# Pairing messages of one bin into double rows before the scatter, in one group of five, in a graph kernel on one core

## The chip, the core and the metric

The kernel runs on one core of a Trainium2 chip. The metric is the device time of one execution in microseconds (us); the figure used is the median of several runs. One further execution is recorded by the hardware profiler; all views below come from it.

## The reference

A graph layer with N = 12,500 nodes of 128 features and 400,000 edges. An edge has a source node `src`, a target `dst` (sorted), 20 attributes and a weight. Cut to what matters:

```python
h    = maximum(layernorm(x), 0) @ W_in2f.T            # one row per node
Wij  = (smu(edge_attr @ W_f1.T + b_f1) @ W_f2.T + b_f2) * edge_weight[:, None]
x_ij = h[dst] * Wij                                   # one message of 128 per edge
agg  = segment_sum(x_ij, src, num_segments=N)         # sum of messages by source node
out  = x + smu(agg @ W_o1.T + b_o1) @ W_o2.T + b_o2
```

`smu` is a smooth activation (Gelu plus a linear part). Edges come sorted by `dst`, so the rows of `h` that a tile needs lie close together; the sum, though, goes by `src`, which is random.

## The kernel before, in words

**Tiles, groups, supers.** 128 edges are a tile, four tiles a group (`GRP`), two groups a super; 3,125 tiles make 782 groups and 391 supers. The nodes are cut into 98 bins of 128.

**Two phases, overlapped.** In the first phase each message is written to a slot of its bin in DRAM: a row of 129 floats (128 values and the node's place within the bin), by one indirect DMA per tile, issued by GpSimd (`scatter_tile`, L812 to L821; the instruction is recorded at L815). In the second phase the slots of a bin are read back 128 rows at a time (`fetch`, L839), VectorE compares the places with a row of numbers to make a 0/1 matrix (`choose`, L860), and TensorE adds all messages of a node by an f32 product with it (`add`, L873); VectorE adds the result to `agg` (L886).

**Parts.** The supers are cut into ten parts (`PARTS`, L33), each with its own capacity per bin (`CAP`, a multiple of 128, from the mean plus 5.8 deviations) and three DRAM buffers used in turn. While the messages of part k are computed and scattered, the slots of part k-1 are read back and summed: `chores` and `parts` spread those products evenly over the groups of the part. With the parts of before, the capacities are 6, 6, 6, 6, 5, 4, 3, 3, 2 and 1 times 128, 42 in all. The first part also carries the setup (layer norm, `h`, weight splitting), as `step` deals it out.

**Kept groups.** The supers of the last two parts (from 368 on, `EARLY`; 23 of them) are computed early, one after every nine others, from the second part on, and their rows are kept in DRAM (`kept_rows`). At the end they are only loaded and scattered. So the first 368 supers are the scattered ones of the main loop (736 groups), and from about 3,700 us on only kept rows are scattered.

**A round.** The main loop (from L1324) has a round per group. The order on each engine is written out by hand; in the round of position p:

- `send(g)` scatters group p (GpSimd, in order), at the top of the round
- `number(p+1)` (L641, VectorE) makes the slot indices; `weigh(p+1)` (L741, L742, TensorE) makes the filter rows into the one `pw` bank
- the first half of the bin sums (L873)
- `mix(p+1)`: ScalarE writes the places (`places_in`, L802 or L804), VectorE multiplies filter and gathered rows into a message buffer `ms` (L754); there are six of them, and one is free again when the scatters that read it have landed
- `gather`, `take` (L697, L716), `hide`, `bend` (L661, L669) and `pick_part` (L552, L553) for groups p+2 and p+3
- `count(p+2)` (L599 to L602, TensorE), `bins(p+3)` (L585, VectorE), `read(p+2)` (L629, VectorE): the slot number of a message is its rank among the messages of its bin. `bins` builds 0/1 rows of 98 bins that are summed along the tiles, `count` adds up within a tile with a triangular matrix, and `read` picks a message's own count by a maximum
- the second half of the bin sums

SyncE issues the loads and the reads of the slots in its own order. Should a count exceed a capacity, a flag in `bad` sends the kernel into a slow repair path at its end.

Of the kernel before, what the change touches and what calls it, by code (L numbers as in the profile page):

```python
# [32 lines left out]
PARTS = (59, 59, 59, 59, 48, 37, 27, 20, 16, 7)  # L33
# [6 lines left out]
ROUND = 12582912.0  # L40


@with_exitstack
def gnn_kernel(
# [46 lines left out]
    for a, n in eps_of:  # L91
        mean = n * SUP * P * P / N
        dev = SIGMA * math.sqrt(mean)
        CAP.append(math.ceil((mean + dev) / P) * P)
        ZMIN.append(max(0, math.floor((mean - dev) / ZP) * ZP) if len(ZMIN) < BUFS else 0)
# [4 lines left out]
    assert all(NB * c < 1 << 24 and c < BIG - 1 for c in CAP)  # L100
# [6 lines left out]
    stores = [dram.tile([NB * CAP[k], ROW], F32, name=f"buf{k}") for k in range(min(BUFS, EPOCHS))]  # L107
    bufs = [stores[k % BUFS][0:NB * CAP[k], :] for k in range(EPOCHS)]
    tab = dram.tile([N + P, D], F32, name="tab")
# [51 lines left out]
    bad = const.tile([P, 4 + 2 * EPOCHS], F32, name="bad")  # L161
# [24 lines left out]
    wls = const.tile([P, P], BF, name="wls")  # L186

# [123 lines left out]
    with tc.tile_pool(name="ld", bufs=4) as ld, \  # L311
# [40 lines left out]
        def head_of(c):  # L352
# [7 lines left out]
            rb = parts_tile().rearrange("p n k d -> p (n k d)").bitcast(U8)[:, :GRP * P].rearrange("p (n e) -> p n e", e=P)  # L360
            z = 0 if c else FEW
            base_f = edge.tile([1, CH // GRP], F32, name="base_f")
# [62 lines left out]
        ds = edge.tile([P, FEW], I32, name="ds", bufs=1)  # L425
        ss = edge.tile([P, FEW], I32, name="ss", bufs=1)
        dsf = edge.tile([P, FEW], F32, name="dsf", bufs=1)
        ssf = edge.tile([P, FEW], F32, name="ssf", bufs=1)
# [67 lines left out]
        loaded, onehot, bins_of, slots, hidden, taken = {}, {}, {}, {}, {}, {}  # L496

# [23 lines left out]
        def targets(s):  # L521
# [3 lines left out]
            rb = ld.tile([P, SUP * P], U8, name="rbc")  # L525
# [39 lines left out]
        def bins(g):  # L565
# [6 lines left out]
            so = cnt.tile([P, GRP, NB], F16, name="so_kept" if kept else "so", bufs=2 if kept else 3)  # L572
# [11 lines left out]
            for j in range(n):  # L584
                nc.vector.scalar_tensor_tensor(so[:, j], irow_ps[:, :NB], hi_f[:, t + j:t + j + 1],  # L585
                                               so[:, j - 1] if j else before, op0=ALU.is_equal, op1=ALU.add)
            last[k] = so[:, n - 1]
            bins_of[g] = (before, so)
# [3 lines left out]
        def count(g):  # L592
# [3 lines left out]
            n = groups[g][1]  # L596
# [3 lines left out]
            if n > 1:  # L600
                nc.tensor.matmul(pc[:, 1:n], rest_h, so[:, :n - 1], start=False, stop=False, skip_group_check=True)  # L601
# [1073 lines left out]
```

## Time and profile before

| | |
|---|---|
| median of 3 runs | 4070.55 us (4062.09 to 4072.97) |
| the profiled execution's own time | 4075.27 us |
| its span in the trace | 4073.5 us |
| indirect scatters | 2944 of computed rows at L815, 181 of kept rows |
| bytes moved by DMA | 891.06 MB |
| mean granted TensorE clock | 0.922 |

The span is the time from the first to the last recorded instruction; the execution's own time lies 1.8 us above it. In the views, PE is TensorE, PEld its weight loads, DVE VectorE, ACT ScalarE, POOL GpSimd. A row of the lines reads: line, engine, operation, output<-inputs, shapes, count, then busy time in us and the mean duration of one in ns, then the idle time of the engine just before them and what ended it. Busy time counts overlapping instructions once, so busy time over count can be less than the mean duration. In the waits, the row names who waited, for whom, the us in total, the times and the longest.

### The profile page before, as it was taken

How to read it: one execution, taken by the hardware profiler on the slowest of the kernel's cores; microseconds unless marked ns; L12 is line 12 of the kernel's file. 1: busy time of each engine (PE TensorE's matmuls, PEld its weight loads, DVE VectorE, ACT ScalarE, POOL GpSimd, SP SyncE). 2: the span in 40 equal slices, each digit the busy share in tenths (PEclk: the TensorE clock that was granted, in tenths of full speed). 3: DMA queues.
4: the chain of work that ended last, by engine and by line, in shares of the span. 5: the costliest groups of instructions: out<-in, count | busy, mean ns of one | idle time of the engine just before them, and what ended most of it. 6: DMA issues, size and time to landing. Idle time of an engine off the chain costs nothing.

```text
span 4073.5 us, 78743 instructions
## 1 busy us (share of the span) xinstructions
PE 3198.0 (79%) x23721; PEld 2666.9 (65%) x24048; DVE 2964.6 (73%) x6883; ACT 2723.2 (67%) x6848; POOL 3066.0 (75%) x3169
## 2 busy tenths in 40 slices
PE   7767767878888788788887788888788788888658
PEld 4345555666667666666766667777677677777547
DVE  7986666777777777777777777777777777777347
ACT  6769877777777677777777777777666666665002
POOL 6777767777777777777777777777777777777776
PEclk9978888998999999989999999999989999989889
DMA  5887778888887767767777768777777877877888
GB/s 163 240 238 198 214 206 241 244 235 234 242 245 217 204 196 216 204 203 207 208 207 220 204 195 231 216 218 221 212 203 216 223 209 226 229 208 200 254 251 252
DMA packets 659740, 891.06 MB, mean 219 GB/s; under 512 B 183268, under 2 KB 460904, under 8 KB 659178
## 3 DMA queue, kind: packets, MB, share of 16 engines
q1 hardware_dynamic: 551881, 666.59, 59.6%
q0 software_dynamic: 100112, 207.06, 15.8%
q10 hardware_dynamic: 7312, 12.29, 0.9%
q8 instruction: 191, 3.13, 0.3%
q14 instruction: 244, 1.99, 0.2%
HBM read 500.66 MB, written 384.95 MB: 217 GB/s over the span
## 4 chain that ended last, share of the span: by engine, by line
DMA 33%; PE 17%; POOL 15%; DVE 15%; issue 11%; ACT 8%; SPq 0%; DVEq 0%; ACTq 0%; POOLq 0%; another core or an unknown queue 0%
DMA buf<-ms,ix 31%; POOL buf L815 15%; PE pw L741 6%; PE pg L873 5%; DVE ms L754 4%; DVE so L585 4%; ACT hg L716 3%; DVE sl L629 1%; DVE se L860 1%; PE ph L697 1%; ACT oh L552 1%; PE pw L742 1%; ACT ge L669 1%; ACT oh L553 1%; PE pc L599 1%
## 5 line engine op out<-in xcount | busy, mean ns | idle before, releaser
L815 POOL DMA_INDIRECT buf<-ms,ix x2944 | 2850.4, 968 | 929.1 <-issue 644.6
L741 PE MATMUL pw<-w_f,ge 128*128 128x128 f32 x5568 | 1099.9, 322 | 501.1 <-DVE ms L754 461.6
L873 PE MATMUL pg<-se,rw 128*128 128x128 f32 x8036 | 1244.4, 296 | 143.4 <-DVE se L860 81.0
L741 PEld LDWEIGHTS pw<-w_f,ge 128*128 128x128 f32 x5568 | 915.6, 207 | 613.0 <-DVE ms L754 433.1
L873 PEld LDWEIGHTS pg<-se,rw 128*128 128x128 f32 x8036 | 1062.6, 203 | 230.6 <-issue 105.1
L754 DVE TENSOR_TENSOR ms<-pw,hg 128x512 f32<-128x512 f32 x696 | 479.3, 689 | 736.8 <-DMA buf<-ms,ix 442.2
L585 DVE SCALAR_TENSOR_TENSOR so<-irow_ps,hi_f,so 128x98 f16<-128x98 f32 x2936 | 931.5, 317 | 78.1
L716 ACT ACTIVATE hg<-ph,w_sb 128x128 f32<-128x128 f32 x2784 | 789.5, 365 | 281.5 <-PE ph L697 272.2
L860 DVE TENSOR_TENSOR se<-irow_ps,rw 128x1536 f32<-128x1536 f32 (+1 forms) x345 | 588.0, 1704 | 148.9 <-DMA rw<-buf 120.2
L742 PE MATMUL pw<-wls,f 128*128 128x128 bf16 x2784 | 642.4, 231 | 0.0
L553 ACT ACTIVATE oh<-oh,onesb 128x512 bf16<-128x512 bf16 x780 | 562.7, 721 | 25.4
L552 ACT ACTIVATE oh<-rbc,nrow 128x512 bf16<-128x512 uint8 x762 | 564.6, 741 | 4.0 <-DMA rbc<-rel_dram 4.0
L629 DVE TENSOR_REDUCE sl<-pc 128x4 f32<-128x392 f32 x782 | 434.9, 556 | 7.1 <-PE pc L602 6.4
L802 ACT ACTIVATE ms<-lo_b,mark 128x4 f32<-128x4 bf16 (+1 forms) x428 | 125.6, 293 | 443.1 <-DMA buf<-ms,ix 417.6
L697 PE MATMUL ph<-hw,oh 126*128 126x128 bf16 x2784 | 294.1, 232 | 64.0 <-ACT oh L553 55.0
L742 PEld LDWEIGHTS <-f 128*128 128x128 bf16 x2784 | 295.4, 106 | 0.0
L697 PEld LDWEIGHTS <-oh 126*128 126x128 bf16 x2784 | 204.1, 104 | 134.8 <-ACT oh L553 119.5
L669 ACT ACTIVATE ge<-pu 128x512 f32<-128x512 f32 x450 | 274.5, 610 | 14.4 <-PE pu L661 13.7
L599 PE MATMUL pc<-so,tri 128*128 128x392 f16 x736 | 255.3, 347 | 24.3 <-DVE sl L629 4.6
L601 PE MATMUL pc<-so,rest_h 128*128 128x294 f16 x736 | 221.2, 300 | 0.0
L815 POOL DMA_INDIRECT buf<-ms,ix_kept x181 | 175.0, 967 | 55.2 <-issue 54.0
L804 ACT ACTIVATE ms<-lo_b 128x4 f32<-128x4 bf16 x353 | 72.4, 205 | 205.8 <-DMA buf<-ms,ix 190.7
(266 smaller groups left out, 2867.2 us busy)
## 6 DMA issues: line engine op xcount, KB each, us to landing
rw<-buf SPq DMA_DIRECT2D x292, 774.0 KB
f<-f_parts SPq DMA_DIRECT2D x370, 240.0 KB
buf<-zero SPq DMA_DIRECT2D x146, 387.0 KB
rbc<-rel_dram SPq DMA_DIRECT2D x389, 128.0 KB
buf<-ms,ix POOLq DMA_INDIRECT x2944
f_parts<-hs SPq DMA_DIRECT2D x105, 360.0 KB
rw<-buf SPq DMA_DIRECT2D x49, 645.0 KB
f_parts<-hs SPq DMA_DIRECT2D x107, 240.0 KB
```

The costliest lines, as they stand in the source:

```text
L552: nc.scalar.activation(oh, loaded[s][1][:, o:o + n], AF.Abs, bias=pneg if s < FEW // SUP else nrow)
L553: nc.scalar.activation(oh, oh, AF.Relu, scale=-1.0, bias=onesb[:, 0:1])
L585: nc.vector.scalar_tensor_tensor(so[:, j], irow_ps[:, :NB], hi_f[:, t + j:t + j + 1], so[:, j - 1] if j else before, op0=ALU.is_equal, op1 ...
L629: nc.vector.tensor_reduce(sl[:, :n], pc[:, :n], op=ALU.max, axis=AX.X)
L697: nc.tensor.matmul(ph[:, j * P:(j + 1) * P], oh[:3 * WIN, a:a + P], hw[:3 * WIN, g % PER, :], start=True, stop=True)
L716: nc.scalar.activation(hg[:, j * P:(j + 1) * P], rows_of[g][:, j * P:(j + 1) * P], AF.Copy, scale=w_sb[:, t + j:t + j + 1])
L741: nc.tensor.matmul(pw[:, a:a + P], ge[:, a:a + P], w_f2, start=True, stop=False)
L742: nc.tensor.matmul(pw[:, a:a + P], fb[:, o + a:o + a + P], wls, start=False, stop=True)
L754: nc.vector.tensor_tensor(ms[:, :n, 0:P], pw.rearrange("p (j f) -> p j f", f=P)[:, :n], hg.rearrange("p (j f) -> p j f", f=P)[:, :n], op=A ...
L815: i = nc.gpsimd.indirect_dma_start(out=bufs[k][:, :], out_offset=bass.IndirectOffsetOnAxis(ap=ix[:, j:j + 1], axis=0), in_=ms[:, j, :], in ...
L860: nc.vector.tensor_tensor(se[:, a:a + n], own.unsqueeze(1).to_broadcast([P, n, P]), rows_in[c][:, a:a + n, P:P + 1].to_broadcast([P, n, P] ...
L873: nc.tensor.matmul(pgs[0][:, g, :], rows_in[c][:, o, 0:P], sel[c][:, o, :], start=(q == 0), stop=(q == Q[k] - 1))
```

## The change

In one group of five (a *paired* group), the messages of tiles 2 and 3 are not scattered as they are. Each looks for a row of tile 0 or 1 of the same bin and the same rank within its bin; if there is one, it moves, by a product with a 0/1 matrix, into a second half of that row. The rows of tiles 0 and 1 then have 258 floats and go to two neighbouring slots, by one indirect DMA for each of the two tiles. The messages of tiles 2 and 3 that found no row (*leftovers*) are gathered by a third 0/1 matrix into one tile of 128 rows, which is scattered with a later group, its *host*, at least four positions on. So a paired group issues two scatters, its host five. A row without a partner has zeros in its second half.

What changes with it:

- the plan of pairs; the parts become 56, 56, 56, 56, 46, 36, 36, 26, 16, 7, and the capacities allow for more slots: 6, 6, 6, 6, 5, 4, 4, 3, 2, 1 times 128. The rows of the main loop stay the first 368 supers.
- `bins`, `count`, `read`, `number`: in a paired group the ranks of tiles 0 and 1 count double, and tiles 2 and 3 are ranked by themselves; one more row of bins in paired and host groups; a fifth count in the host
- new functions `spread_keys`, `match`, `rank_left`, `place_left`, `permute`, `take_pairs`, called in the rounds p and p+1
- `mix` splits the product of a paired group in two and writes places, bins and slot bases for the moved half
- fewer buffers: `rbc` 3 instead of 4, `mt` 2 of 6 x 128 columns instead of 3 of 4 x 128; the head's small tiles share others

The diff, cut to its core:

```diff
-PARTS = (59, 59, 59, 59, 48, 37, 27, 20, 16, 7)
+PARTS = (56, 56, 56, 56, 46, 36, 36, 26, 16, 7)
+EVERY = 5
+WIDER = 0.17
...
+        for p, g in enumerate(seq):
+            if g // PER >= EARLY:
+                continue
+            since_pair += 1
+            if wanting and p >= wanting[0][0] + 4:
+                host[g] = wanting.pop(0)[1]
+            elif since_pair >= EVERY and g > BY and g + 10 < ends_of[epoch[g // PER]]:
+                paired[g] = len(paired)
+                wanting.append((p, g))
+                since_pair = 0
...
+            if g in paired:
+                last[k] = so[:, GRP]
+                nc.vector.scalar_tensor_tensor(so[:, GRP], so[:, 1], 2.0, before, op0=ALU.mult, op1=ALU.add)
+            if g in host:
+                last[k] = so[:, GRP]
+                nc.vector.scalar_tensor_tensor(so[:, GRP], irow_ps[:, :NB], left_of[host[g]][1], so[:, GRP - 1],
+                                               op0=ALU.is_equal, op1=ALU.add)
...
+            if g in paired:
+                nc.tensor.matmul(pc[:, :n], tri2, so[:, :n], start=True, stop=False, skip_group_check=True)
+                nc.tensor.matmul(pc[:, 1:n:2], both2, so[:, 0:n:2], start=False, stop=False, skip_group_check=True)
+                nc.tensor.matmul(pc[:, :n], ones_h, before.unsqueeze(1).to_broadcast([P, n, NB]), start=False, stop=True,
+                                 skip_group_check=True)
...
+        def spread_keys(g):
+            kt = ps1.tile([P, GRP * P], F32, name="pt")
+            for j in range(2):
+                nc.tensor.transpose(kt[:, j * P:(j + 1) * P], keys_of[g][:, j:j + 1].to_broadcast([P, P]), ident)
...
+        def match(g):
+            kt, key = matched[g], keys_of.pop(g)
+            pp = edge.tile([P, 6 * P], F32, name="mt", bufs=2)
...
+            for i in range(2):
+                nc.vector.scalar_tensor_tensor(pp[:, i * 2 * P:(i + 1) * 2 * P].rearrange("p (j e) -> p j e", j=2),
+                                               kt[:, :2 * P].rearrange("p (j e) -> p j e", j=2), key[:, 2 + i:3 + i],
+                                               onesb.unsqueeze(1).to_broadcast([P, 2, P]),
+                                               op0=ALU.is_equal, op1=ALU.mult, accum_out=had[:, i:i + 1])
+            i = paired[g]
+            nc.vector.tensor_scalar(alone[:, 2 * i:2 * i + 2], had, -1.0, 1.0, op0=ALU.mult, op1=ALU.add)
...
+        def rank_left(g):
...
+            nc.tensor.matmul(at_, tri, alone[:, i:i + 2], start=True, stop=False, skip_group_check=True)
+            nc.tensor.matmul(at_[:, 1:2], ones_h, alone[:, i:i + 1], start=False, stop=True, skip_group_check=True)
...
+        def place_left(g):
...
+            nc.vector.tensor_scalar(at_, kt[:, 2 * P:2 * P + 2], -BIG, None, op0=ALU.add)
+            nc.vector.tensor_tensor(pp[:, 4 * P:].rearrange("p (j e) -> p j e", j=2),
+                                    irow_ps.unsqueeze(1).to_broadcast([P, 2, P]),
+                                    at_.unsqueeze(2).to_broadcast([P, 2, P]), op=ALU.is_equal)
...
+        def permute(g):
+            pp, cd = matched.pop(g)[1], apart_of.pop(g)
+            po = ps1.tile([P, GRP * P], F32, name="pt")
+            for j in range(3):
+                w = ROW + 2 if j == 2 else ROW
+                for i in range(2):
+                    o = (4 + i if j == 2 else 2 * i + j) * P
+                    nc.tensor.matmul(po[:, j * (ROW + 2):j * (ROW + 2) + w], pp[:, o:o + P], cd[:, i, :w],
+                                     start=(i == 0), stop=(i == 1))
...
+        def take_pairs(g):
...
+            nc.vector.tensor_scalar(at_[:, 0:1], po[:, o + ROW:o + ROW + 1], NOBIN, None, op0=ALU.add)
+            nc.vector.tensor_scalar(at_[:, 1:2], po[:, o + ROW + 1:o + ROW + 2], NOBIN_ROW, drow[:, k:k + 1],
+                                    op0=ALU.add, op1=ALU.min)
+            nc.scalar.activation(ms[:, 1::2, :], po[:, :o].rearrange("p (j r) -> p j r", j=2)[:, :, 0:ROW], AF.Copy)
+            nc.scalar.activation(lt, po[:, o:o + ROW], AF.Copy)
...
+                    nc.vector.tensor_tensor(cd[:, :, 0:P], pw[:, 2:], hg[:, 2:], op=ALU.mult)
+                    nc.vector.tensor_tensor(ms[:, 0::2, 0:P], pw[:, :2], hg[:, :2], op=ALU.mult)
...
+            if g in paired:
+                for j in range(2):
+                    scatter_rows(g, ms[:, 2 * j:2 * j + 2].rearrange("p j r -> p (j r)"), ix[:, j:j + 1])
+                return
             for j in range(groups[g][1]):
                 scatter_tile(g, ms, ix, j)
+            if g in host:
+                scatter_rows(g, left_of.pop(host[g])[0], ix[:, GRP:])
...
             if p >= SLACK:
-                if by_edge(g):
+                if by_edge(g) and g not in paired:
                     send(g)
...
             weigh(at(p + 1))
+            if at(p + 1) in paired:
+                spread_keys(at(p + 1))
...
             mix(at(p + 1))
+            if g in paired:
+                permute(g)
+                take_pairs(g)
+                send(g)
+            if at(p + 1) in paired:
+                match(at(p + 1))
...
             bins(at(p + 3))
+            if at(p + 1) in paired:
+                rank_left(at(p + 1))
             read(at(p + 2))
+            if at(p + 1) in paired:
+                place_left(at(p + 1))
```

More of the change, by code (lines that the diff above doesn't have):

```diff
@@ L40 @@
 ROUND = 12582912.0
+NOBIN = 200.0
+NOBIN_ROW = float(1 << 17)
 @with_exitstack
@@ L99, in gnn_kernel @@
     SPAN = [ROWS // q for q in Q]
-    assert all(NB * c < 1 << 24 and c < BIG - 1 for c in CAP)
+    assert all(NB * c + P < NOBIN_ROW and c < BIG - 1 for c in CAP)
     const = ctx.enter_context(tc.tile_pool(name="const", bufs=1))
@@ L605, in count @@
                 pt = ps1.tile([P, GRP * P], F32, name="ph")[:, :NB]
-                nc.tensor.matmul(pt, ones_h, so[:, n - 1], start=True, stop=True)
+                nc.tensor.matmul(pt, ones_h, after, start=True, stop=True)
                 mm = cnt.tile([P, 2], F32, name="mm")
@@ L613, in count @@
                 pt = ps1.tile([P, GRP, P], F32, name="ph")[:, 0, :NB]
-                nc.tensor.matmul(pt, ones_h, so[:, n - 1], start=True, stop=True)
+                nc.tensor.matmul(pt, ones_h, after, start=True, stop=True)
                 mm = cnt.tile([P, 2], F32, name="mm")
```

144 lines of the change are left out of this document (110 added, 34 removed).

## The prediction

> **What bounds the kernel now.** I read the page's busy shares first, then GpSimd's scatter line in stretches of time, then the waits, then durations. On the page, four engines stand close together, and one number alone does not pick the bound.
>
> ```profile
> span 4073.5 us, 78743 instructions
> ...
> PE 3198.0 (79%) x23721; PEld 2666.9 (65%) x24048; DVE 2964.6 (73%) x6883; ACT 2723.2 (67%) x6848; POOL 3066.0 (75%) x3169
> ```
>
> In the second view, the windows of the scatter line, see the count in brackets: about 79 scatters in 100 us, in the middle and near the end alike, while the DMA share goes from 0.70 to 0.97.
>
> ```profile
> 1800.00:1900.00 100.00, 76.21 (x79) 0.93 0.70 201
> ...
> 3800.00:3900.00 100.00, 76.09 (x79) 0.91 0.97 292
> ```
>
> The timeline gives the pitch: from the first row below to the last lie 11 scatters.
>
> ```profile
> 4000.51 0.95 POOL L815 DMA_INDIRECT buf<-ms,ix_kept  x1 [0.30 <-issue]
> ...
> 4014.40 0.96 POOL L815 DMA_INDIRECT buf<-ms,ix_kept  x1 [0.30 <-issue]
> ```
>
> 13.89 / 11 = 1.263 us for each scatter of 128 rows. 3125 scatters at 1.263 are 3947 us of the 4073.5. **GpSimd's issue of scatters is the bound** from start to 4014 us; a scatter fewer is worth 1.263 us as long as GpSimd always finds the next one ready.
>
> Does it? The waits between 600 and 3700 us say how far ahead the others are.
>
> ```profile
> PE pw L741 <- DVE ms L754: 409.4, 258, 9.4
> DVE ms L754 <- DMA buf<-ms,ix: 409.3, 179, 10.8
> ...
> DVE ms L754 <- ACT ms L804: 139.3, 49, 7.7
> ```
>
> VectorE's product waits for a message buffer that an old scatter must free (409.3, and 139.3 through ScalarE's wait for the same), and TensorE waits for the product. That is back pressure: the compute side is ahead, and held. How far ahead is what decides this change.
>
> **The change part by part.** *Removed: scatters.* By the rule of the plan, the new parts of 56, 56, 56, 56, 46, 36, 36, 26 pair 10, 21, 21, 21, 17, 13, 13 and 9 groups: 125. Each drops two scatters and gives its host one, so 125 are saved of 3125: 125 x 1.263 = 158 us, 145 of them (115 groups) after the first part. I price a scatter of 258 floats a row like one of 129. The trace shows no such scatter: 128 rows at 1.263 us is one bound, and two narrow scatters for one wide one, 2.53 us, the other. I take the first, since the rate above does not move with what the DMA engines do; the row count stays 128. The other is a rival. The bytes grow by 125 leftover tiles of 66 KB, 8 MB: hidden, by the same rows. By the drawn indices at most 106 of a group's 256 moved messages stay over, so one scatter of 128 takes them.
>
> *Added on VectorE and the others, per paired group.* The prices, from the lines between 600 and 3700 us, and the last two rows from the lines of the whole span:
>
> ```profile
> L873 PE MATMUL pg<-se,rw 128*128 128x128 f32 x6756 | 1071.8, 296 | 46.6 <-DVE agg L886 38.9 <-DVE agg L884 7.3
> ...
> L873 PEld LDWEIGHTS pg<-se,rw 128*128 128x128 f32 x6756 | 898.6, 201 | 112.5 <-DVE agg L886 58.3 <-issue 15.8 <-DVE agg L884 10.8
> ...
> L585 DVE SCALAR_TENSOR_TENSOR so<-irow_ps,hi_f,so 128x98 f16<-128x98 f32 x2437 | 773.4, 317 | 64.8
> L716 ACT ACTIVATE hg<-ph,w_sb 128x128 f32<-128x128 f32 x2446 | 693.5, 365 | 214.6 <-PE ph L697 209.3 <-DVE so L585 2.2 <-issue 1.3
> ...
> L754 DVE TENSOR_TENSOR ms<-pw,hg 128x512 f32<-128x512 f32 x611 | 420.6, 688 | 627.1 <-DMA buf<-ms,ix 409.3 <-ACT ms L804 139.3 <-PE pw L742 17.8
> L629 DVE TENSOR_REDUCE sl<-pc 128x4 f32<-128x392 f32 x657 | 365.4, 556 | 6.8 <-PE pc L602 6.0
> ...
> L599 PE MATMUL pc<-so,tri 128*128 128x392 f16 x611 | 210.2, 344 | 18.4 <-issue 1.5 <-DVE so L585 0.9 <-DVE sl L629 0.8
> ...
> L601 PE MATMUL pc<-so,rest_h 128*128 128x294 f16 x611 | 182.8, 299 | 0.0
> ...
> L802 ACT ACTIVATE ms<-lo_b,mark 128x4 f32<-128x4 bf16 (+1 forms) x415 | 121.8, 293 | 422.5 <-DMA buf<-ms,ix 397.0 <-issue 23.9 <-DMA sm<-in_f_t 1.1
> L641 DVE SCALAR_TENSOR_TENSOR ix<-sl,hic 128x4 int32<-128x4 f32 x611 | 98.2, 161 | 9.5
> ```
> ```profile
> L764 DVE SCALAR_TENSOR_TENSOR mt<-pw,b,hg 128x512 f32<-128x512 f32 x39 | 29.2, 748 | 16.7 <-ACT hg L720 16.6
> ...
> L777 PE MATMUL pt<-ident,mt 128*128 128x128 f32 x156 | 26.4, 293 | 33.0 <-DVE mt L764 31.9 <-DVE prow L130 1.0
> ```
>
> VectorE: 98 elements cost 317 ns and 512 cost 748, so 1.04 ns an element and 0.48 us for 256; a plain product of 512 is 0.69, so 0.42 for 256. Two more count rows (paired and host) 0.63; two matching passes 0.96; the product in two halves 0.15 more; place matrix 0.42; host's reduce of 490 instead of 392 columns 0.10; six small ones (key, alone, rank, two leftover places, host index) at 0.16, 0.96. Sum 3.2 us. TensorE, by busy time over count (1071.8 / 6756 = 0.159 for half an f32 product): six 0/1 products, 12 halves, 1.9; two transposes at 26.4 / 156 = 0.17, 0.34; 2 x 196 more count columns at (344 - 299) / 98 = 0.46 ns, 0.18; two tiny rank products, 0.1 (at that slope, starts only). 2.5 us. ScalarE: three place copies at 0.29, and moving 258 and 129 columns out of PSUM at about 0.44 and 0.365: 1.7 us.
>
> *Bins read back.* The caps become 43 rows of 128 in place of 42 per bin: 98 more f32 products, 196 halves x 0.159 = 31 us of TensorE over 122 fives of groups, 0.25 each. TensorE's bill is 2.75 us per pair.
>
> *Moved.* A paired group's two scatters are issued in the middle of its round, after the 0/1 products, where others are issued at the top. GpSimd's queue holds the scatters of several earlier groups (six message buffers), so two microseconds there are hidden; without that backlog every pair would cost them. Two waits are new in line: VectorE's leftover places wait for the last 0/1 product (behind it stand the next count rows and the reduce), TensorE's key transposes for VectorE's indices. Fewer buffers for `rbc` and `mt` I cost at nothing: the load for three supers ahead needs a one-hot that ScalarE wrote two rounds before; if not, SyncE's reads queue behind it.
>
> **The sum, in a five of groups.** The busy times of a window (TensorE, its weight loads, VectorE, ScalarE, GpSimd, with counts), of the long stretch and of 36 us in it:
>
> ```profile
> 600.00:3700.00 3100.00, 2510.57 (x19422) 2144.84 (x19719) 2308.60 (x5312) 2184.29 (x5521) 2357.12 (x2437) 0.94 0.77 218
> ...
> 1220.00:1256.00 36.00, 33.85 (x283) 29.77 (x289) 31.50 (x73) 28.04 (x71) 27.46 (x29) 1.00 0.78 201
> ```
>
> Today 20 scatters take 20 x 3100 / 2437 = 25.44 us; with 19, 1.27 less. So per five the compute side must find 1.27 + 3.2 = 4.5 us on VectorE, and 1.27 + 2.75 = 4.0 on TensorE (ScalarE, 17.9 of 25.44 us busy now, would be 19.6 of 24.2: not the bound). What it has spare, three ways. (a) TensorE's wait, 409.4 us over 611 groups: 3.35 per five. (b) VectorE's, 409.3 + 139.3: 4.49 per five. (c) A stretch where nothing held the product, in VectorE's timeline:
>
> ```profile
> 1222.76 0.68 DVE L754 TENSOR_TENSOR ms<-pw,hg 128x512 f32<-128x512 f32 x1
> ...
> 1244.68 0.69 DVE L754 TENSOR_TENSOR ms<-pw,hg 128x512 f32<-128x512 f32 x1
> ```
>
> Six rounds in 21.92 us, 3.65 a round. A five holds 5 x 657 / 611 = 5.38 rounds (the kept groups are computed too), 19.6 us: 5.8 spare. The granted clock stood at 1.00 there against 0.94 over the whole.
>
> The three disagree around the demand: by (a) TensorE is 0.67 short, by (b) VectorE just covers it, by (c) all is covered. I take (b), the middle, and charge 0.3 for the new waits in line: 0.97 us kept per five, x 115 = 112 us.
>
> *The first part* goes the other way. There ScalarE and VectorE carry the setup too, and GpSimd is already starved:
>
> ```profile
> 100.00:600.00 500.00, 368.33 (x379) 0.86 0.77 219
> ```
>
> 500 us would hold 395 scatters; 16 are missing, 20 us. Ten pairs at 3.2 us of VectorE find no slack there: 32 us of work, less what the back pressure of the early groups hides; the setup falls on 112 instead of 118 groups. I charge 25 us and credit no scatter. The end (kept groups at 79 per 100 us) is untouched.
>
> Sum: 4075.27 (the profiled run's own time) - 112 + 25 = 3988, **3990 us**. The median of the runs shown is 4070.55, 0.1% lower. With (a) it is 115 x 0.6 = 69 gained, 4031; with (c) 145 gained, 3955.
>
> **The rivals.**
> *The compute side keeps pace everywhere.* For it: stretch (c). Against: the first part. Time 3955 with the charge for the first part, 3917 without. The Trainium skill (Trainium Kernel Development and Optimization, Performance Expectations) says that matmul busy time misleads, since matmuls overlap, and that weight-load busy time tells. In this trace weight loads are busy 2144.84 of 3100 us; with 12 more halves at 898.6 / 6756 = 0.133 us and about 0.8 for the others they would come to (17.6 + 2.4) / 24.1 = 0.83 of the time, what stretch (c) shows (29.77 of 36): by that rule TensorE is no bound, and the time is 3955.
> *Slower: the hand-over between VectorE and TensorE.* Keys, transposes, matching, ranks, places, products, leftover places alternate between the two, in order on both, through a single `pw` and a single `pt` bank. If their bills add up instead of lying side by side, 3.2 + 2.75 = 5.95 us stand against TensorE's spare 3.35. From 3.35 - 25 / 115 = 3.1 us upward the kernel is slower. Half way between 2.75 and 5.95, at 4.35, a five takes 26.44: 115 x 1.0 + 25 lost, 4215. Against it: matching lies beside weights and counts on TensorE. For it: in stretch (c) VectorE is busy 31.50 of 36 us and TensorE 33.85, so both are nearly full when nothing holds them.
> *A wide scatter costs two.* If 258 floats a row are issued as two rows, the change doesn't cut what GpSimd issues: 250 wide ones at 2.53 and 125 leftovers give +125 x 1.263 = 158, 4233. The Trainium skill (DMA: Bandwidth & Descriptors, Anatomy of one DMA) calls descriptor generation a small part of a DMA's fixed cost; no run here shows it for wide rows.
> *Gain and bill cancel*, about 4065.
>
> **How the numbers follow.** Forecast (3955 to 4045) 0.48; pace kept 0.14; cancel 0.10; hand-over 0.22; wide scatter 0.06. A measurement tells about 0.3%, 12 us, from no change. Faster: 0.48 + 0.14 + 0.02 of the cancelling case = 0.64; within: 0.08 + 0.02 of the hand-over = 0.10; slower: 0.20 + 0.06 = 0.26. Range 3925 to 4110: about 0.04 is left out below, the wide scatter and 0.10 of the hand-over above.
>
> **What would show it.** Wide scatters at the same 0.96 us and pitch. 3000 scatters. If pace is kept, still 79 per 100 us and some wait of the product for buffers; if not, fewer than 79, that wait gone, and VectorE or TensorE above 90% busy. In the first part fewer scatters per 100 us than now. Wrong: GpSimd idle for VectorE or ScalarE for more than some 100 us in all, or a wide scatter above 1.3 us.

## The result, and the profile after

| | kernel before | changed kernel |
|---|---|---|
| median of 4 runs each | 4071.76 us (4062.09 to 4073.04) | 4015.4 us (4014.04 to 4017.36) |
| ratio | | 0.9867 [0.985, 0.9884] |
| span of the profiled execution | 4073.5 us | 4012.3 us |
| indirect scatters | 3125 | 3000 |

The change takes 1.3% off, 56 us. The prediction had 3990 us, 82 us less than this median before. The direction and the bound hold, and the gain is about two thirds of the forecast.

From the page of the changed kernel, the span, the busy shares and the costliest group (scatters are recorded at L959 now):

```profile
span 4012.3 us, 85549 instructions
...
PE 3315.2 (83%) x25912; PEld 2821.8 (70%) x26245; DVE 3264.7 (81%) x8658; ACT 2837.0 (71%) x7473; POOL 2949.5 (74%) x3044
...
L959 POOL DMA_INDIRECT buf<-ms,ix x2694 | 2611.9, 970 | 944.3 <-issue 653.0
```

VectorE went from 73% to 81% and TensorE from 79% to 83%, in a shorter span. GpSimd went from 75% to 74%. On the page, then, the engine that was called the bound is now less busy than both of them. What that means is read in two stages. The windows of the changed kernel (TensorE, its weight loads, VectorE, ScalarE, GpSimd, each with its count, then granted clock, DMA share, GB/s):

```profile
100.00:600.00 500.00, 359.29 (x1960) 254.56 (x1982) 354.14 (x1081) 369.92 (x954) 315.94 (x326) 0.81 0.68 202
600.00:3600.00 3000.00, 2572.53 (x21335) 2248.10 (x21632) 2579.39 (x6932) 2297.60 (x6118) 2263.85 (x2336) 0.98 0.79 230
```

*The long stretch.* 2336 scatters in 3000 us are one in 1.284 us, against 3100 / 2437 = 1.272 before. The rate is nearly kept while each pair of groups brings one scatter less. 115 saved scatters at 1.272 are 146 us; 2336 scatters that come 0.012 us later each give 28 back; 118 us remain.

*The first part.* From 100 to 600 us there are 326 scatters, where 379 stood before. By 600 us the changed kernel is 53 scatters behind, only ten of them saved ones; the other 43, at 1.263 us, are 54 us. 118 - 54 = 64 us, and the spans differ by 61.2.

The windows of the scatter line, 100 us each, changed kernel:

```profile
300.00:400.00 100.00, 58.20 (x60) 0.81 0.57 168
...
500.00:600.00 100.00, 60.12 (x62) 0.82 0.61 186
600.00:700.00 100.00, 76.21 (x79) 0.88 0.75 227
...
1800.00:1900.00 100.00, 75.99 (x79) 0.98 0.74 216
2600.00:2700.00 100.00, 70.34 (x74) 0.97 0.75 215
```

Most windows of the long stretch still hold 79, GpSimd's own pace. A few hold 74 to 76: there GpSimd found nothing ready. Where it stood still, GpSimd's timeline shows. The longest pause between 600 and 3600 us:

```profile
2600.78 0.95 POOL L959 DMA_INDIRECT buf<-ms,ix  x1 [0.30 <-issue]
2608.31 0.95 POOL L959 DMA_INDIRECT buf<-ms,ix  x1 [6.58 <-issue]
```

There are twelve pauses of more than half a microsecond in that time. Nine of them, 24 us together, stand at one and the same place in the order: just ahead of a paired group's two wide scatters (two or three narrow ones of the next group go first). The other three come to 3 us. So the 28 us by which the scatters come later are, nearly all of them, pauses ahead of pairs. A paired group's rows are made in the middle of its round, and at these places GpSimd had no earlier group left to issue.

Who waits has changed. The waits of the changed kernel from 600 to 3600 us:

```profile
ACT ms L759 <- DVE lat L757: 257.1, 100, 6.1
...
PE pt L705 <- DVE key L687: 77.8, 79, 2.3
PE pt L726 <- DVE h_first L719: 73.5, 48, 4.7
DVE lat L756 <- PE pt L746: 66.8, 62, 2.5
...
PE pw L859 <- DVE ms L889: 48.4, 57, 5.1
...
DVE ms L889 <- DMA buf<-ms,ix: 32.1, 26, 3.0
```

The last two rows are those that carried the old bound. TensorE's wait for the product fell from 409.4 (in 3100 us) to 48.4 us (in 3000), and the product's wait for a buffer from 409.3 to 32.1. The compute side is hardly held back by scatters any longer. In the place of these waits stand the first four rows above, all new, all of them steps of the pairing that TensorE, VectorE and ScalarE hand to each other.

And a wide scatter costs what a narrow one does. The scatter line between 600 and 3600 us (duration in ns, least, median, most), changed kernel, 2224 scatters beside the leftovers' 112, some 224 of them wide:

```profile
L959 POOL DMA_INDIRECT buf<-ms,ix x2224: 952/958/1487, 599.3 to 3599.1; - x186
```

The same view of the kernel before, 600 to 3700 us:

```profile
L815 POOL DMA_INDIRECT buf<-ms,ix x2437: 954/958/1483, 599.8 to 3699.7; - x188
```

None took more than 1.49 us, where two narrow ones take 2.53, and the longest before was as long. In the trace a wide scatter can be told by its DMA packets, 32 of 4,128 bytes in place of 16. Counted off in that order, the 224 wide ones take 0.96 us in the median and 0.970 in the mean, as the narrow ones do, and the next scatter starts 1.26 us behind them in the median.

### The profile page after: what moved, and what is told of

It reads as the page before. It is cut to its first block, busy times and chain, and to the rows that moved or that the text cites. A ratio compares the mean times of both kernels' runs of the same rounds, so it can differ in the third digit from the quotient of the medians.

```text
span 4012.3 us, 85549 instructions
## 1 busy us (share of the span) xinstructions
PE 3315.2 (83%) x25912; PEld 2821.8 (70%) x26245; DVE 3264.7 (81%) x8658; ACT 2837.0 (71%) x7473; POOL 2949.5 (74%) x3044
## 4 chain that ended last, share of the span: by engine, by line
PE 24%; DVE 16%; DMA 16%; ACT 11%; issue 9%; POOL 8%; SPq 1%; DVEq 0%; ACTq 0%; POOLq 0%
DMA buf<-ms,ix 12%; PE pg L1017 8%; POOL buf L959 8%; PE pw L859 6%; DVE so L614 4%; ACT hg L834 4%; DVE ms L889 3%; PE pt L746 2%; DVE se L1004 2%; ACT oh L578 2%; DVE sl L671 2%; ACT ge L787 2%; PE ph L815 2%; ACT oh L579 1%; DVE mt L714 1%
## 5 line engine op out<-in xcount | busy, mean ns | idle before, releaser
L959 POOL DMA_INDIRECT buf<-ms,ix x2694 | 2611.9, 970 | 944.3 <-issue 653.0
L859 PE MATMUL pw<-w_f,ge 128*128 128x128 f32 x5568 | 1025.8, 307 | 109.1 <-DVE ms L889 79.1
L859 PEld LDWEIGHTS pw<-w_f,ge 128*128 128x128 f32 x5568 | 880.6, 199 | 169.4 <-ACT ge L787 67.3
L614 DVE SCALAR_TENSOR_TENSOR so<-irow_ps,hi_f,so 128x98 f16<-128x98 f32 x2693 | 855.3, 318 | 73.9
L889 DVE TENSOR_TENSOR ms<-pw,hg 128x512 f32<-128x512 f32 x571 | 392.2, 687 | 202.2 <-ACT hg L834 81.4
L671 DVE TENSOR_REDUCE sl<-pc 128x4 f32<-128x392 f32 (+1 forms) x782 | 448.5, 573 | 11.8 <-PE pc L644 7.0
L759 ACT ACTIVATE ms<-pt 128x258 f32<-128x258 f32 x125 | 48.3, 386 | 312.5 <-DVE lat L757 283.8
L641 PE MATMUL pc<-so,tri 128*128 128x392 f16 (+1 forms) x611 | 211.5, 346 | 21.5 <-DVE sl L671 4.8
L959 POOL DMA_INDIRECT buf<-ms,ix_kept x181 | 176.0, 972 | 55.2 <-issue 53.7
L787 ACT ACTIVATE ge<-pg 128x512 f32<-128x512 f32 (+1 forms) x334 | 204.8, 613 | 0.0
L746 PE MATMUL pt<-cd,mt 128*128 128x129 f32 x1500 | 201.2, 286 | 0.9 <-DVE at L733 0.5
```

Source lines behind the costliest of these rows:

```text
L671: nc.vector.tensor_reduce(sl[:, :n], pc[:, :n], op=ALU.max, axis=AX.X)
L787: nc.scalar.activation(ge[:, :n], units_of[g][:, :n], AF.Gelu, scale=ZS)
L859: nc.tensor.matmul(pw[:, a:a + P], ge[:, a:a + P], w_f2, start=True, stop=False)
L959: i = nc.gpsimd.indirect_dma_start(out=(wide if g in host or g in paired else bufs)[k][:, :], out_offset=bass.IndirectOffsetOnAxis(ap=ix, ...
```

## The experiments

The theory after the result: a scatter is worth its pitch where GpSimd is the bound. In the long stretch the bill of a pair brings the compute side level with GpSimd, so little is left to gain there. The forecast missed because the first part lost about twice what was charged. Rivals: the loss comes from the fewer buffers and shared tiles, all along the kernel; or the new waits in line set the pace of the long stretch; or scatters are not the price at all. All ratios are to the kernel before, on the same chip.

**The change in pieces.** Three kernels, run together (kernel before: 4081.68 us).

The changed kernel without pairs in the first part:

```diff
-            elif since_pair >= EVERY and g > BY and g + 10 < ends_of[epoch[g // PER]]:
+            elif since_pair >= EVERY and epoch[g // PER] > 0 and g + 10 < ends_of[epoch[g // PER]]:
```

> The changed kernel, but no group of the first part is paired: 115 pairs in place of 125. My theory: the ten pairs of the first part cost about half of the 53 us that the changed kernel is behind there (42 scatters fewer done by 600 us than the ten saved explain), since ScalarE, VectorE and TensorE carry the setup there and have no slack; then the time falls by 15 to 35 us, to 3980 to 4000 us, and more scatters are done by 600 us. Rival: the shorter first part alone (56 supers in place of 59, the setup dealt out more densely) or the fewer buffers cost it all; then ten scatters more are issued for nothing and the time rises by 0 to 13 us, to 4015 to 4028.

The kernel before with the new sizes of the parts:

```diff
-PARTS = (59, 59, 59, 59, 48, 37, 27, 20, 16, 7)
+PARTS = (56, 56, 56, 56, 46, 36, 36, 26, 16, 7)
```

> The kernel before with the ten part sizes of the changed one and nothing else. My theory: the shorter first part makes the setup denser, by 6%, where GpSimd is already starved, and costs 10 to 30 us: 4080 to 4100. Rival: the sizes don't matter (the setup has room in the rounds), 4065 to 4077, and the loss of the first part belongs to pairs or buffers.

The changed kernel with no pair at all (its parts, buffers and shared tiles stay; the few instructions behind the loop that look whether the leftovers of a group were more than 128 go with the pairs):

```diff
-            elif since_pair >= EVERY and g > BY and g + 10 < ends_of[epoch[g // PER]]:
+            elif False:
```

> The changed kernel with an empty plan of pairs: its part sizes, capacities, its fewer buffers and its shared tiles, but every group scattered as before, 3125 scatters. My theory: beside the part sizes (the run of the kernel before with these sizes) buffers and shared tiles cost nothing measurable, so this run is within 10 us of that one, and both are 10 to 30 us above the kernel before. Rival: the fewer buffers hold up the loads, and this run is more than 15 us above the one with the sizes alone.

| | us | ratio |
|---|---|---|
| new part sizes alone | 4105.09 | 1.0055 [1.0041, 1.0068] |
| changed, no pairs | 4108.29 | 1.0064 [1.005, 1.0077] |
| changed, no pairs in the first part | 4007.33 | 0.9806 [0.9791, 0.9821] |
| changed (first measurement) | 4015.4 | 0.9867 [0.985, 0.9884] |
| changed (again, on the chip of the next set) | 4028.36 | 0.9873 [0.9855, 0.989] |

Read downwards, in per cent of some 4075 us, and with the mean of the last two, 0.987: part sizes cost 22 us; buffers and shared tiles 4, within their intervals nothing; the 115 pairs behind the first part give 105 (93 to 117 from the ends of the two intervals); the ten pairs of the first part cost 26 (12 to 40 from the ends of their intervals). Each step is a difference of neighbours, so they add up to the whole by construction; what is measured is each size. As differences, all three runs came out as expected; as times, 4007.33 and 4105.09 lie 7 and 5 us above what was expected, and the kernel before took some 10 us more on that chip. The rival of the buffers falls.

Where the part sizes cost is seen in the scatters issued by 600 us. The windows of the index tile (VectorE, then GpSimd with its count). Kernel before:

```profile
0.00:600.00 600.00, 17.61 (x113) 428.54 (x441) 0.87 0.74 210
```

New part sizes alone:

```profile
0.00:600.00 600.00, 17.08 (x109) 414.80 (x424) 0.85 0.73 206
```

Changed, no pairs:

```profile
0.00:600.00 600.00, 16.81 (x108) 413.88 (x422) 0.85 0.74 205
```

Changed kernel:

```profile
0.00:600.00 600.00, 16.45 (x111) 377.06 (x388) 0.84 0.66 196
600.00:1200.00 600.00, 20.70 (x143) 452.12 (x467) 0.96 0.85 251
```

From 441 to 424 by the part sizes alone: 17 scatters at 1.263 are 21 us, the 22 that the run was slower. From 422 to 388 by ten pairs: 34 fewer, ten of them saved; 24 are 30 us, against 26 by the times. What a pair does to GpSimd there is in the waits of the changed kernel from 100 to 600 us:

```profile
POOL buf L959 <- issue: 101.2, 202, 8.5
...
DVE cd L877 <- ACT hg L834: 29.1, 10, 5.7
POOL buf L959 <- ACT ms L759: 26.5, 3, 12.9
```

Three waits, up to 12.9 us long, are put down to the moved rows (L759). In GpSimd's timeline they are three of ten of a kind. Two of the ten:

```profile
291.39 0.96 POOL L959 DMA_INDIRECT buf<-ms,ix  x1 [0.31 <-issue]
300.89 0.95 POOL L959 DMA_INDIRECT buf<-ms,ix  x1 [8.54 <-issue]
...
323.63 0.95 POOL L959 DMA_INDIRECT buf<-ms,ix  x1 [0.30 <-issue]
337.44 0.96 POOL L959 DMA_INDIRECT buf<-ms,ix  x1 [12.85 <-ACT ms L759]
```

All ten pairs of the first part have such a pause, 19 scatters from one to the next, 2.0 to 12.9 us long and 67 us together, where 0.3 each is usual. The scatter behind each pause is a narrow one of the group after the pair, and the two wide ones are the third and fourth. So it is not the moved rows alone that are late: by this order, GpSimd gets nothing to issue for most of the paired group's round. That is the case that the prediction named as "without that backlog every pair would cost them". It costs less than its 67 us. Between 100 and 600 us all pauses of more than half a microsecond come to 93 us in the changed kernel, to 45 in the one without these ten pairs and to 19 in the kernel before, and ten scatters less have to be issued. L877, the product split for a pair, waited 29.1 us for ScalarE in ten waits, as many as there are pairs.

**Is a scatter the price?** The kernel before, with the last tile of one group in five not counted and not scattered, 137 scatters in all; nothing is added:

```diff
+        def thin(g):
+            return g > BY and s_of(g) < EARLY and g % 5 == 0
...
-                nc.vector.scalar_tensor_tensor(so[:, j], irow_ps[:, :NB], hi_f[:, t + j:t + j + 1],
+                bin_of = eps if thin(g) and j == n - 1 else hi_f[:, t + j:t + j + 1]
+                nc.vector.scalar_tensor_tensor(so[:, j], irow_ps[:, :NB], bin_of,
...
-            for j in range(groups[g][1]):
+            for j in range(groups[g][1] - thin(g)):
```

> The kernel before, with the last tile of one group in five (137 groups of the main loop after the fiftieth) left out of the count and of the scatter, so its messages are missing from the sums; all other work stays. My theory: GpSimd's issue is the bound and the compute side has at least 3.35 us to spare in five groups against the 1.27 that it must find here, so all 137 are saved but the few in the first part: 137 x 1.263 = 173 us at most, 150 to 173 us faster, 3898 to 3921. Rival: the compute side holds the pace already, and little is gained: 4000 or more.

3917.62 us, 0.9597 [0.9584, 0.961]: 164 us of the 137 x 1.263 = 173, 1.20 us for a scatter. Scatters are the price; at this rate the change's 125 would bring 150 us if its pairs cost nothing.

**Is the compute side full after the change?** The next set ran on another chip (kernel before: 4076.58 us). The changed kernel stood in it as it is:

> The changed kernel once more, beside the next runs on one chip, as their reference. Expected: the ratio of the first measurement, 0.987, within 0.003.

4028.36 us, 0.9873 [0.9855, 0.989]. Beside it, the changed kernel without the 125 leftover scatters; the leftovers are not counted either, and all else is computed as before:

```diff
-                nc.vector.scalar_tensor_tensor(so[:, GRP], irow_ps[:, :NB], left_of[host[g]][1], so[:, GRP - 1],
+                nc.vector.scalar_tensor_tensor(so[:, GRP], irow_ps[:, :NB], eps, so[:, GRP - 1],
...
-                scatter_rows(g, left_of.pop(host[g])[0], ix[:, GRP:])
+                left_of.pop(host[g])
```

> The changed kernel with the 125 leftover scatters left out (the leftovers are not counted and their messages are missing from the sums); all compute stays. My theory: the compute side is now close to its own limit (the product's waits for buffers fell from 548 to about 32 us, TensorE's for the product from 409 to 50), so little of 125 x 1.263 = 158 us is gained: 30 to 80 us, ratio 0.967 to 0.98. Rival: the compute side still keeps pace (rounds of 3.65 us, as in the free stretch of the kernel before), and 130 us or more are gained in the main loop, ratio 0.955 or less.

3983.44 us, 0.9761 [0.9744, 0.9777]. Against 0.9873 for the changed kernel on this chip that is 46 us for 125 scatters, where GpSimd as the only bound would give 158. The same cut that was worth 1.20 us each in the kernel before is worth 0.37 here. The compute side is full, or as good as.

**How long does the compute side need by itself?** In both kernels the last tile of every scattered group after the 50th is left out (in the changed kernel not of paired groups), so that GpSimd has 15 scatters, 18.9 us, per five groups and waits for the others.

```diff
+            return g > BY and s_of(g) < EARLY
```

and in the changed kernel

```diff
+            return g > BY and s_of(g) < EARLY and g not in paired
```

The first time, these two ran on a chip on which the kernel before took 5461.56 us, a third more than on any other here.

> The kernel before, with the last tile of every group of the main loop after the fiftieth left out of count and scatter (three scatters a group, 18.9 us of GpSimd per five groups), so a quarter of their messages is missing; all compute stays. It measures what the compute side does alone, so it tells apart the three slacks of the prediction, as us per five scattered groups in the main loop: by (a), TensorE's wait, 22.1; by (b), VectorE's wait, 21.0; by (c), the free stretch, 19.6. Expected (b), and a time of 3590 to 3680 us; by (a) about 3720, by (c) about 3450.

> The changed kernel with the same left out (the last tile of every group that is not paired, after the fiftieth; 18.9 us of GpSimd per five). The difference to the run of the kernel before with the same left out is the bill of a pair on the compute side. My theory: 23.9 us per five groups, as in the run without leftovers (there GpSimd needs 22.7), so that run was compute-bound, and the bill is about 3.0 us per pair; GpSimd's 24.0 and this are neck and neck. Rival: much faster than 23.9, then the run without leftovers was still held by GpSimd or by the order of the scatters.

4545.75 us, 0.8315 [0.8278, 0.8351], and 5162.21 us, 0.9435 [0.9396, 0.9474]. All three kernels were slow on that chip. In the first of the two traces, 130.3 us of ScalarE's idle time between 1200 and 2400 us are put down to `remote`, which is another core or an unknown queue. Why the chip was slow stays open, and these two times tell nothing of the question. They were repeated on another chip (kernel before: 4076.84 us).

> The same as the run of the kernel before with the last tile of each later group left out, since in that series the kernel before itself took 5462 us on its chip, a third more than elsewhere. Expected where it takes its usual 4060 to 4085: by slack (b) 21.0 us per five groups in the main loop and 3590 to 3680 us; by (a) 22.1 and about 3720; by (c) 19.6 and about 3450.

> The same for the changed kernel with the last tile of each later group that is not paired left out. Expected where the kernel before takes its usual time: 23.9 us per five groups in the main loop, a bill of about 3.0 us per pair against the run beside it. Rival: much less than 23.9, then GpSimd or the order of the scatters still held the run without leftovers.

3589.45 us, 0.88 [0.8785, 0.8814], and 3948.5 us, 0.9685 [0.9669, 0.9701]. The windows of the index tile, kernel before with fewer scatters:

```profile
1200.00:3200.00 2000.00, 75.33 (x472) 1379.55 (x1418) 0.98 0.85 240
...
1200.00:3200.00 2000.00, 1824.96 (x15210) 1594.73 (x15441) 1788.89 (x4113) 1677.33 (x4249) 1379.55 (x1418) 0.98 0.85 240
```

The second row has all its engines, in the order given above. 1418 / 3 = 472.7 groups in 2000 us: **21.2 us for five groups** is the compute side of the kernel before. The three readings of its slack in the prediction made 22.1 (a), 21.0 (b) and 19.6 us (c) of 25.44. Reading (b), the one taken, is the nearest. The time, 3589.45, lies just under the 3590 to 3680 expected for it, far from the 3720 of (a) and the 3450 of (c).

The same windows of the changed kernel with fewer scatters, and all its engines over the same time:

```profile
1200.00:3400.00 2200.00, 79.08 (x546) 1337.20 (x1380) 0.98 0.77 217
...
1200.00:3400.00 2200.00, 1931.27 (x16182) 1696.44 (x16407) 1940.12 (x5202) 1721.83 (x4576) 1337.20 (x1380) 0.98 0.77 217
```

1380 / 3 = 460 groups in 2200 us: **23.9 us for five**. The place matrix, one for each pair (L738 in this kernel), in the lines of this stretch:

```profile
L738 DVE TENSOR_TENSOR mt<-irow_ps,at 128x256 f32<-128x256 f32 x86 | 36.5, 425 | 3.0
```

460 groups at 2000 / 472.7 = 4.23 us would be 1946 us; 254 us are more, for 86 pairs: 3.0 us a pair. The forecast's bill was 3.2 on VectorE and 2.75 on TensorE. Reckoned in the same way from the two rows of all engines, VectorE's busy time grew by 2.3 us a pair, TensorE's by 1.8 and ScalarE's by 1.0. So a pair takes some 0.6 us more than the busy time that it adds to the engine that it loads most. What else can take them is waiting between the engines; the rows do not say at which hand-over.

For the changed kernel as it is, the same stretch:

```profile
1200.00:3400.00 2200.00, 77.36 (x535) 1659.60 (x1713) 0.98 0.77 224
```

1713 scatters and 85 saved ones are 1798 / 4 = 449.5 groups: 24.47 us for five (over 600 to 3600 us, with 2336 scatters and 112 pairs, 24.51), where the forecast had 25.44 - 0.97 = 24.47. GpSimd alone would need 1713 x 1.263 us for them, 24.07; the compute side alone 23.9. Two limits 0.7% apart, and together they take 0.4 us more than the later one. Not all of this comes from their being level. The kernel before with one tile in five groups left out has about as many scatters, and a compute side that needs only 21.2:

```profile
1200.00:3200.00 2000.00, 66.03 (x414) 1521.67 (x1568) 0.96 0.78 219
```

1568 / 19 x 5 = 412.6 groups, 24.24 us for five, and GpSimd alone would need 19 x 1.263 = 24.0: 0.24 us are lost there too. The other 0.2 us are some 20 us over the long stretch, the size of the pauses ahead of the pairs. The two limits are felt at some distance as well: without the leftovers, GpSimd alone would need 22.9 us, and five groups take 24.2 (1646 scatters and 85 pairs in the same 2200 us), 0.3 above the compute side alone.

**Do the new waits in line set the pace?** Two more of that set. First a version whose first part is as long as before, without pairs in it:

```diff
-PARTS = (56, 56, 56, 56, 46, 36, 36, 26, 16, 7)
+PARTS = (59, 56, 56, 56, 45, 36, 36, 24, 16, 7)
...
-        paired = n if len(CAP) < len(eps_of) - SENT_LAST else 0
+        paired = n if 0 < len(CAP) < len(eps_of) - SENT_LAST else 0
```

> The changed kernel with the first part as it was before, 59 supers and no pair in it (the other parts 56, 56, 56, 45, 36, 36, 24, 16, 7). If the loss of the first part is its density (the part sizes alone measured +0.55%) plus its ten pairs (0.6% between the changed kernel and the run without them), both go: ratio 0.973 to 0.978, 35 to 55 us under the changed kernel. Rival: the 0.55% of the part sizes come from another part than the first (more slots read back); then only the ten pairs' share is gained, ratio 0.979 to 0.983.

3989.37 us, 0.9782 [0.9763, 0.98], between the two spans expected. The first 600 us:

```profile
0.00:600.00 600.00, 17.48 (x113) 429.73 (x442) 0.87 0.76 210
600.00:1200.00 600.00, 20.03 (x138) 438.39 (x454) 0.94 0.87 246
```

442 scatters by 600 us, as before the change: by that count the first part is repaired. In time, 0.9873 - 0.9782 are 37 us of the 48 that the part sizes and the ten pairs cost. The rest is lost right behind it: from 600 to 1200 us there are 454 scatters, where the changed kernel has 461 on this chip and had 467 on the first. What is late there wasn't tried, and stays open.

Then, in that version, the keys are spread (L705) behind the first half of the bin sums in place of ahead of it, so that TensorE need not wait for VectorE's keys:

```diff
-            if at(p + 1) in paired:
-                spread_keys(at(p + 1))
...
             parts(lo + (hi - lo) // 2)
+            if at(p + 1) in paired:
+                spread_keys(at(p + 1))
             mix(at(p + 1))
```

> The run with the long first part, and the two key transposes moved behind the first half of the bin sums on TensorE, so that they no longer wait for VectorE's keys (80 us of TensorE's idle time in the changed kernel's main loop). Theory that GpSimd is the bound for all but some 30 us of the main loop: at most 0 to 15 us under the run with the long first part. Rival, that the hand-over between TensorE and VectorE sets the pace: 40 us or more under it.

3986.34 us, 0.9773 [0.9759, 0.9786], 3 us under the one without, within the noise. The waits of this version from 600 to 3600 us:

```profile
PE pt L726 <- DVE h_first L719: 96.6, 87, 3.5
DVE lat L756 <- PE pt L746: 72.8, 61, 5.4
...
PE pt L705 <- DVE key L687: 27.5, 34, 1.7
```

The same view without the move:

```profile
DVE lat L756 <- PE pt L746: 68.6, 59, 5.0
PE pt L705 <- DVE key L687: 68.5, 75, 2.3
PE pt L726 <- DVE h_first L719: 66.3, 49, 3.3
```

The wait for the keys fell by 41 us, and the next hand-over rose by 30. The wait for the keys, then, does not set the pace: most of it came back one step later, and no time was won. That the chain of hand-overs as a whole costs time is not refuted by this, since the run moved a wait and took hardly any away; the 0.6 us a pair above speak for it. A version that issues the paired group's rows a round later, with a backlog in front of them, was not run either. Of all kernels with the whole computation this and the one without the move were the fastest.

## Why the prediction was right, and which term was mis-sized

*The bound, and the price of a scatter.* Right. Taken out alone, scatters were worth 1.20 us each; the pitch of 1.263 us stayed; wide ones take 958 ns like narrow ones.

*The bill of a pair.* Right in its sum, within a tenth: 3.0 us measured in the kernel that waits for the compute side. In its parts that is luck to some extent: the engines' busy times grew by less than their bills (VectorE 2.3 us against 3.2, TensorE 1.8 against 2.75), and what fills up the 3.0 is, as far as the rows show, waiting between the engines. From the lines of the changed kernel between 600 and 3600 us, where a row shows an added step:

```profile
L746 PE MATMUL pt<-cd,mt 128*128 128x129 f32 (+1 forms) x1344 | 172.2, 278 | 0.3 <-ACT oh L578 0.3
...
L714 DVE SCALAR_TENSOR_TENSOR mt<-pt,key,onesb 128x256 f32<-128x256 f32 x226 | 99.5, 478 | 10.6 <-PE pt L705 10.3
...
L734 DVE TENSOR_TENSOR mt<-irow_ps,at 128x256 f32<-128x256 f32 x113 | 48.0, 425 | 3.9
...
L877 DVE TENSOR_TENSOR cd<-pw,hg 128x256 f32<-128x256 f32 x113 | 47.2, 417 | 9.6 <-ACT hg L834 6.1 <-PE pw L860 3.1
...
L714 DVE DVE_READ_ACCUMULATOR mt<-pt,key,onesb 128x1 f32 x226 | 18.9, 84 | 0.0
```

Matching took 0.478 us a pass where 0.48 was forecast, the place matrix 0.425 for 0.42, the half product 0.417 for 0.42. The 0/1 products took 172.2 / 112 = 1.54 us a pair in place of 1.9. Not foreseen: each matching pass with a sum along the row brings a read of the accumulator of 84 ns, 0.17 us a pair. The single prices of VectorE are good, then, and their sum is still above what its busy time grew by: busy time counts overlapping instructions once, and a sum of durations does not.

*Slack by VectorE's wait.* Right: 21.0 us forecast for the compute side, 21.2 measured, so 4.3 us of slack in place of 4.49. TensorE's wait for the product (a) undercounts; the stretch in which nothing held the product (c) overcounts. Why (a) does was not tried. The waits were read at a granted clock of 0.94 and the 21.2 measured at 0.98, so that (b) came out this close is in part luck.

*The long stretch.* 112 us were forecast, 105 measured by the runs, 118 by the count of scatters. The bound, the slack and the size hold. The 0.3 us a five for the new waits in line were a guess of about the right size; what takes them are the pauses of GpSimd ahead of a pair, which the prediction held to be hidden by the backlog ("Moved").

*The first part.* This is the term that failed: "Ten pairs at 3.2 us of VectorE find no slack there: 32 us of work, less what the back pressure of the early groups hides; the setup falls on 112 instead of 118 groups. I charge 25 us and credit no scatter." Both causes were named, but they were charged as one. Measured: 22 us for the part sizes and 26 for the ten pairs, with 4 for the buffers 52 in place of 25. So the 25 us are about what the pairs alone cost, and the denser setup came on top. With the measured sizes, 4075.27 - 105 + 52 = 4022 us, 0.2% from the median measured.

*The rivals.* "A wide scatter costs two" is refuted by the duration and the rate. The slower hand-over is refuted in its price: bills that add up would be 5.95 us a pair, 4.35 half way; 3.0 were measured. Its mechanism is there in part: of the 2.3 us that VectorE and the 1.8 that TensorE were busy longer, at least 1.1 lay side by side. "The compute side keeps pace everywhere" is refuted: with 125 scatters less the changed kernel gains only 46 us. With it falls the use that the prediction made of weight-load busy time. The Trainium skill (Trainium Kernel Development and Optimization, Performance Expectations) names it as a good metric of how close a kernel is to roofline. Here, in the kernel that waits for its compute side, weight loads are busy 1696.44 of 2200 us, 0.77: the distance to a full TensorE may be read from that, but not that TensorE and VectorE together could go faster.

*The signs.* "VectorE or TensorE above 90% busy" was too high a bar. In that same row VectorE is busy 1940.12 / 2200 = 88% and TensorE 1931.27 / 2200 = 88%, and the pace is theirs. "GpSimd idle for VectorE or ScalarE for more than some 100 us in all" was meant as a sign of being wrong, and came near: 67 us in ten pauses of the first part and 24 in nine of the long stretch, all ahead of pairs, though on whom GpSimd waited there is shown for few of them. The profile puts down most of these to "issue" and not to an engine, so the rows of the waits do not show it.

## What to carry to other kernels

When a change trades instructions of the bounding engine for work elsewhere, look for the wait by which the bound holds the others back, at the engine that meets it first; here VectorE's wait for a buffer gave the compute side's pace within 0.2 us in 21. When the sum brings the two sides level, count on losing a little more than the later of the two (here 0.4 us in 24, of which 0.24 were lost with slack behind the bound as well), and on little further gain from the bound's side alone (here 46 us of 158). Look for the pauses where the change moves an issue of the bounding engine to a later point of its round. Price every stage in which the bound is already starved by itself, and each cause in it by itself: the same pair that gained 0.9 us in the long stretch (105 / 115) cost 2.6 in the first part (26 / 10).

## What the runs showed of the hardware

*TensorE's clock rises as its waits go.* The granted clock from 600 us on was 0.94 in the kernel before (600 to 3700 us) and 0.98 after (600 to 3600 us), and in the two versions of the kernel before with fewer scatters 0.96 and 0.98 (1200 to 3200 us). It fell from 0.86 to 0.81 in the first part (100 to 600 us), where TensorE got through fewer matmuls (1960 against 2044). The Trainium skill (TensorE: Matmul & The Clock Gate, Part 1: The HAM clock gate) says that the clock is set by how busy TensorE has been just before. The long stretch agrees: waits of up to 9.4 us for the product went, and the clock came. The first part does not settle it: TensorE was busy for 359.29 us there, against 349.76 before. The prediction's sum held no such change of the clock; what it gave in us was not measured.

*The rate of indirect scatters* depended here neither on their width (129 or 258 floats a row) nor on how busy the DMA engines were (79 in 100 us at a DMA share of 0.70 and of 0.97 before, and of 0.74 and 0.75 after).

*A chip can be a third slower* for the same kernel (5461.56 against some 4076 us on the others), and the ratio between kernels isn't the same there. Ratios from different chips stand in one sum only, that of the ten pairs of the first part, where two chips agree on the changed kernel.
